# First attention: turning the weighted values with VectorE's 32-square transpose in place of TensorE products with the identity

## The chip, the cores and the metric

The kernel runs on one core of one Trainium2 chip. The metric is device time in microseconds (us) of one execution. The kernel before takes 1176.46 us, the median of three runs between 1171.67 and 1180.38. The profiled execution has a span of 1177.1 us.

Engines are named as in the profile: PE is TensorE (PEld its weight loads), DVE is VectorE, ACT is ScalarE, POOL is GpSimd, SP is the engine whose queue issues most of the DMA. L400 is line 400 of the kernel.

## The reference

The whole program is two layers, each an attention followed by a mixture of experts, on x of 4 batches x 1024 tokens x 256 channels. Only the first attention is touched. Cut to it:

```python
h = _layernorm(x) * (1 + ca) + sa
Q = (h @ Wq.T).reshape(b, t, 16, 16)                 # 16 heads of 16
q_lat = einsum('bthd,hdl->bthl', Q, q_to_latent)     # latent size 64
logits = einsum('bthl,bsl->bhts', q_lat, h @ Wk_down.T) / sqrt(64)
attn = softmax(where(causal, logits, -1e30))
ctx = einsum('bhts,bsl->bhtl', attn, h @ Wv_down.T)
heads = einsum('bhtl,hld->bthd', ctx, v_up)
x = x + ga * (heads.reshape(b, t, 256) @ Wout.T)
```

After it each row of x is normalised again, sent to 2 of 16 experts, and so on. All data is float32.

## The kernel before

**Tiling.** The weights are folded first, so each head has 16 values per token. A batch's heads are worked in four parts: two groups `g` of 128 channels, and within each two halves `o` (the even and the odd heads). A part holds four heads `hh`, one in each quadrant of 32 partitions. The scores are made transposed: keys on partitions, queries along the free axis. A part has nine *units* (`UNITS`), each of 512 query columns of scores for all four heads, so there are 4 x 2 x 2 x 9 = 144 units in all. For a unit PE makes the scores (`ps_s`, L377), ACT takes the exponential (`pT`, L385) and POOL zeroes the part above the diagonal (L388). Two units later PE multiplies with the values (`ps_av`, L457). The values are stored 32 wide: 16 values and then ones, so that the sum of the weights comes out beside the weighted values.

**Where the change sits.** `ps_av` is one PSUM bank (pool `ps_o`, one buffer) of 128 partitions x 512 queries. Its partition is 32 x head + value index, its column is the query. A part fills it twice (`qc` = 0 and 1: the first and the second 512 queries). Two things have to follow: division by the sum, which in this layout lies in another partition than the values, and the output projection, whose stationary operand needs channels on partitions. The kernel before does this in two turns over the identity. First (`finish`, L396 to L408) DVE copies `ps_av` to `oT` (L464), PE turns it in four products with the identity (`ps_oT`, L400), and DVE takes the reciprocal of the sums (L403) and multiplies (L407), which leaves `on` with tokens on partitions. Then (`project`, L410 to L437) for each two tiles of 128 tokens PE turns `on` back in four products with the identity (`ps_onT`, L417), DVE copies the result to `onT` (L426), PE multiplies with the gated output weights (`ps_out`, L431) and DVE adds it to x (L436). Over four batches that is 32 times `finish` and 16 rounds of `project`.

**Order.** `sums()` emits the products of `ps_av` in the order of the parts. Everything beside the scores and sums is a *task*: a generator that yields after each piece (1 or 0.5 a piece). The tasks are `prepare` (normalisation, values, queries and keys of the next group), `finish`, `project`, the rows and routing for the experts (`rows`), and the sort of the routed rows (`sort`). After each unit `k.around.step(...)` runs one piece, and two on every third unit of the batches after the first (L490). Each call of `step` also advances one *rider*: the sending of sorted rows by POOL's indirect DMAs (L944), which begins when `sort` of the first two batches is done. A scheduler places instructions within each engine's queue from there; POOL's queue follows the written order. Each engine works off its queue in order.

**What stands at the end of the attention.** After the last unit come the last sums, the last `finish`, and `project` of batch 3. Then the expert stage begins with `ps_xT` (L1193), which needs the sorted rows of the first two batches to have been sent and read back.

Of the kernel before, what the change touches and what calls it, by code (L numbers as in the profile page):

```python
# [8 lines left out]
F32 = mybir.dt.float32  # L9
I32 = mybir.dt.int32  # L10
AF = mybir.ActivationFunctionType
ALU = mybir.AluOpType
# [3 lines left out]
P = 128  # L16
B, N, C = 4, 1024, 256
NT = N // P
CC = C // P
H, D, L = 16, 16, 64  # L20
# [44 lines left out]
def bcast(ap, axis, n):  # L65

    shape = list(ap.shape)
    shape.insert(axis, n)
    return ap.unsqueeze(axis).to_broadcast(shape)
# [171 lines left out]
def attention0(ctx, k, a, after_batch=lambda b: None):  # L241

    nc = k.nc
    k.scalar_norm = False

    wp = ctx.enter_context(k.tc.tile_pool(name="a0_w", bufs=1, reuse_waits="tile"))
    vs, ons, qs = ([None, None] for _ in range(3))
    par = wp.tile([P, 2], F32, tag="par", name="par")
    wo = wp.tile([P, CC, C], F32, tag="wo", name="wo")
    for i in (1, 0):  # L250
        if i:
            vs[i] = wp.tile([P, NT, H, 32], F32, tag="v1", name="v1")
        ons[i] = wp.tile([P, NT, C], F32, tag=f"on{i}", name=f"on{i}")
        qs[i] = [wp.tile([P, N], F32, tag=f"{n}{i}", name=f"{n}{i}") for n in ("qT", "kT0_", "kT1_")]
    k.xn = wp.tile([P, 4, C], F32, tag="ln_xn", name="ln_xn")
    wq, wk, wv = (wp.tile([P, CC, C], F32, tag=n, name=n) for n in ("wq", "wk", "wv"))
# [29 lines left out]
    misc = Spread()  # L286
# [39 lines left out]
    recs = k.recs  # L326
# [3 lines left out]
    def prepare(b, g):  # L330

        if g == 0:
            yield from layer_norm_steps(k, b, hT, 0, misc, "m")
            for t in range(0, NT, 2):
                ps = misc.tile([P, 2, C], F32, name="ps_v")
                for i in range(2):
                    for cc in range(CC):
                        nc.tensor.matmul(  # L338
                            ps[:, i, :], lhsT=hT[:, cc, (t + i) * P : (t + i + 1) * P],
                            rhs=wv[:, cc, :], start=cc == 0, stop=cc == CC - 1,  # L340
                        )
                nc.scalar.copy(
                    vs[b % 2][:, t : t + 2, :, :D], ps.rearrange("p t (h d) -> p t h d", d=D)
                )
                yield 1
        else:
            gates[b] = spread_rows(k, work, 0, GATE, 0, "gate_a0", b, 1)[:, 0]
        qT, *kTs = qs[g]
        for w in (wq, wk):
            for hf in range(2):  # L350
                ps = misc.tile([P, 512], F32, name="ps_qk")
                for cc in range(CC):
                    nc.tensor.matmul(  # L353
                        ps, lhsT=w[:, cc, g * P : (g + 1) * P],
                        rhs=hT[:, cc, hf * 512 : (hf + 1) * 512],
                        start=cc == 0, stop=cc == CC - 1,
                    )
                cols = slice(hf * 512, (hf + 1) * 512)
                if w is wq:
                    nc.vector.tensor_copy(qT[:, cols], ps)  # L360
                else:
                    for o in range(2):
                        nc.vector.tensor_scalar(  # L363
                            kTs[o][:, cols], ps, par[:, o : o + 1], None, ALU.mult
                        )
                yield 1
        ready[b, g] = qT, kTs
# [25 lines left out]
            pTs.append(pT)  # L393
        return pTs

    def finish(b, g, o, qc, oT, on):  # L396

        pt = misc.tile([P, 4, P], F32, name="ps_oT")
        for i in range(4):
            nc.tensor.transpose(pt[:, i], oT[:, i * P : (i + 1) * P], k.ident)  # L400
        pt = pt.rearrange("p i (j d) -> p i j d", d=32)
        rec = recs[:, 8 * b + 4 * g + 2 * o + qc]
        nc.vector.reciprocal(rec, pt[:, :, :, D])  # L403
        heads = on[:, 4 * qc : 4 * qc + 4, g * P : (g + 1) * P].rearrange(
            "p t (j o d) -> p o t j d", o=2, d=D
        )
        nc.vector.tensor_tensor(heads[:, o], pt[:, :, :, :D], bcast(rec, 3, D), ALU.mult)  # L407
        yield 1  # L408

    def project(b, on):  # L410
        wg = work.tile([P, CC, C], F32, tag="wg", name="wg", bufs=1)
        nc.vector.tensor_tensor(wg, wo, bcast(gates.pop(b), 1, CC), ALU.mult)
        for t in range(0, NT, 2):
            pt = misc.tile([P, 2, CC, P], F32, name="ps_onT")
            for i in range(2):
                for cc in range(CC):
                    nc.tensor.transpose(  # L417
                        pt[:, i, cc, :], on[:, t + i, cc * P : (cc + 1) * P], k.ident
                    )
            if misc.early:  # L420
                onT = work.tile([P, 2, 512], F32, tag="pT", name="onT", bufs=7)[:, 0, :].rearrange(
                    "p (i c n) -> p i c n", c=CC, n=P
                )
            else:
                onT = work.tile([P, 2, CC, P], F32, tag="onT", name="onT", bufs=1)
            nc.vector.tensor_copy(onT, pt)  # L426
            yield 1
            py = misc.tile([P, 2, C], F32, name="ps_out")
            for i in range(2):
                for cc in range(CC):  # L430
                    nc.tensor.matmul(  # L431
                        py[:, i, :], lhsT=onT[:, i, cc, :], rhs=wg[:, cc, :],
                        start=cc == 0, stop=cc == CC - 1,
                    )
            xs = k.x[b][:, t : t + 2, :]
            nc.vector.tensor_tensor(xs, xs, py, ALU.add)  # L436
            yield 1  # L437
# [5 lines left out]
    around = k.around.tasks  # L443

    def sums():

        for b in range(B):
            on = ons[b % 2]
            for g in range(2):
                for o in range(2):  # L450
                    for qc, pieces in enumerate(SUMS):
                        po = ps_o.tile([P, 512], F32, tag="o", name="ps_av")
                        for n, (u, i) in enumerate(pieces):
                            yield place[b, g, o, u]
                            kb, _, c0, w, _ = UNITS[u][i]
                            for hh in range(4):
                                nc.tensor.matmul(  # L457
                                    po[32 * hh : 32 * hh + 32, 512 - w :],
                                    lhsT=vs[b % 2][:, kb, 8 * g + 2 * hh + o, :],
                                    rhs=exps[b, g, o, u][hh // 2][:, hh % 2, c0 : c0 + w],  # L460
                                    start=n == 0, stop=n == len(pieces) - 1,
                                )
                        oT = work.tile([P, 512], F32, tag="oT", name="oT")
                        nc.vector.tensor_copy(oT, po)  # L464
                        around.insert(0, finish(b, g, o, qc, oT, on))
            projects.append(project(b, on))
            around.append(projects[-1])
            after_batch(b)
# [6 lines left out]
    with k.tc.manual_schedule(engines={mybir.EngineType.Pool}):  # L475
        summing = sums()
        wanted = next(summing)
        for n, (b, g, o, u) in enumerate(units):
            if n == 8:
                k.clear_rows()  # L480
            if (o, u) == (0, 0):
                while (b, g) not in ready:
                    k.around.step(rides=0)
                coming = (b, 1) if g == 0 else (b + 1, 0)
                if coming[0] < B:
                    around.insert(0, prepare(*coming))
            while wanted is not None and wanted <= n - 2:
                wanted = next(summing, None)
            exps[b, g, o, u] = scores(b, g, o, u)
            k.around.step(2 if b and n % 3 == 2 else 1)  # L490
        misc.early = True
        for _ in summing:
            pass
        while projects[-1] in around:
            k.around.step(rides=2)
# [1468 lines left out]
def two_layers(ctx: ExitStack, tc: tile.TileContext, a: dict, out: bass.AP):  # L1964
# [83 lines left out]

    load_x(0)
    again = stages(attention0, attention1, True)  # L2050


# [73 lines left out]
```

## Time and profile before

| | PE | DVE | ACT | POOL |
|---|---|---|---|---|
| busy, us of 1177.1 | 1022.0 | 642.4 | 611.9 | 331.4 |
| share of the span | 87% | 55% | 52% | 28% |

| time | us |
|---|---|
| median of three runs | 1176.46 |
| first scores of the attention to the first `ps_xT` of the experts | about 52 to 569.24 |
| PE busy between 52 and 546 | 478.5 of 494 |

A busy share is an average over stages. What matters for a change inside the attention is which engine is never without work there, and which waits end last between two of its instructions. In the lines that follow, a row of the timeline merges equal instructions that follow each other: start, length, engine, line, operation, tiles written and read, count, and in brackets how long the engine had been idle and what released it. A float32 product is recorded as two matmuls, a turn over the identity as one.

### The profile page before, as it was taken

What the parts mean: (1) busy time and instruction counts of PE and PEld (TensorE: products, weight loads), DVE (VectorE), ACT (ScalarE), POOL (GpSimd) and SP (SyncE); (2) the same over time, 40 slices, a digit from 0 to 9 for tenths busy, and PEclk for the clock granted to TensorE, in tenths of its full rate; (3) what the DMA queues carried; (4) which work ended last, traced back from release to release, by engine and by line L of the source; (5) the groups of instructions that cost most, each with busy time, mean ns of one, the idle gap of its engine ahead of it and who ended that gap; (6) DMA issues with size and microseconds to landing.
All of it is one profiled execution on the core that took longest, in us unless ns stands there. A gap on an engine that the chain in (4) does not pass through costs nothing.

```text
span 1177.1 us, 19004 instructions
## 1 busy us (share of the span) xinstructions
PE 1022.0 (87%) x6350; PEld 607.1 (52%) x6350; DVE 642.4 (55%) x2143; ACT 611.9 (52%) x986; POOL 331.4 (28%) x528
## 2 busy tenths in 40 slices
PE   4999999999999998998688999887798798868771
PEld 2533434343444433443567888776465555546651
DVE  5822233422362144441776787896589978685352
ACT  0377645664457445474264757655664745523331
POOL 1122222220112122466104604420461100542732
PEclk9999999999999998998889999998899899889986
DMA  6992000100010000264744655531421501357863
GB/s 190 347 346 82 1 1 1 41 1 1 1 37 24 1 1 1 68 218 176 299 126 158 208 165 170 158 108 54 143 77 35 193 1 45 104 162 226 275 223 107
DMA packets 99017, 134.63 MB, mean 114 GB/s; under 512 B 8744, under 2 KB 86088, under 8 KB 98400
## 3 DMA queue, kind: packets, MB, share of 16 engines
q1 hardware_dynamic: 86528, 98.97, 25.3%
q0 software_dynamic: 11776, 33.57, 9.3%
q8 instruction: 54, 0.88, 0.3%
q10 hardware_dynamic: 608, 0.79, 0.2%
q14 instruction: 51, 0.42, 0.1%
HBM read 69.55 MB, written 63.75 MB: 113 GB/s over the span
## 4 chain that ended last, share of the span: by engine, by line
PE 66%; DVE 16%; DMA 6%; ACT 5%; issue 4%; POOL 1%; DVEq 0%; SPq 0%; POOLq 0%; ACTq 0%
PE ps_av L457 13%; PE ps_s L377 12%; PE ps_y L1282 6%; PE ps_qk L353 5%; PE ps_k L1472 4%; PE ps_h L1216 4%; DMA ys<-results,index 3%; PE ps_v L338 3%; PE ps_out L431 3%; PE ps_pr L1570 2%; PE ps_q L1498 2%; PE ps_oT L400 2%; PE ps_y L1893 2%; DMA xs<-sorted 2%; PE ps_lnT L1034 1%
## 5 line engine op out<-in xcount | busy, mean ns | idle before, releaser
L385 ACT ACTIVATE pT<-ps_s 128x1024 f32<-128x1024 f32 x288 | 278.8, 1021 | 199.8 <-PE ps_s L377 197.2
L388 POOL TENSOR_SCALAR_AFFINE_SELECT pT<-pT 128x256 f32<-128x256 f32 x256 | 101.1, 414 | 394.3 <-ACT pT L385 390.3
L457 PE MATMUL ps_av<-pT,v 128*32 128x512 f32 (+3 forms) x1536 | 180.0, 509 | 3.3 <-POOL pT L388 3.3
L377 PE MATMUL ps_s<-qT,kT 32*128 32x512 f32 (+3 forms) x1536 | 181.7, 524 | 0.5 <-ACT pT L385 0.5
L954 POOL DMA_INDIRECT ys<-results,index x96 | 100.7, 1048 | 139.5 <-DVE st L1227 35.1
L944 POOL DMA_INDIRECT sorted<-hs,index x96 | 96.9, 1009 | 142.5 <-PE ps_y L1282 67.6
L377 PEld LDWEIGHTS ps_s<-qT,kT 32*128 32x128 f32 x1536 | 75.8, 186 | 99.3 <-issue 80.2
L1282 PE MATMUL ps_y<-w,act 128*128 x376 | 93.2, 404 | 20.1 <-ACT act L1265 20.0
L1240 ACT ACTIVATE hid<-hid,nmr,rstd 128x256 f32<-128x256 f32 x94 | 49.0, 595 | 83.8 <-DVE nmr L1236 83.7
L1282 PEld LDWEIGHTS ps_y<-w,act 128*128 128x128 f32 x376 | 74.1, 202 | 33.4 <-ACT act L1265 22.9
L1216 PE MATMUL ps_h<-w,xT 128*128 x376 | 87.8, 386 | 1.6 <-ACT xT L1199 1.5
L457 PEld LDWEIGHTS ps_av<-pT,v 128*32 128x32 f32 x1536 | 41.0, 110 | 90.7 <-issue 64.5
L464 DVE COPY oT<-ps_av 128x512 f32<-128x512 f32 x32 | 22.0, 689 | 114.6 <-PE ps_av L457 114.6
L1216 PEld LDWEIGHTS ps_h<-w,xT 128*128 128x128 f32 x376 | 70.5, 193 | 11.5 <-ACT xT L1199 2.3
L1893 PE MATMUL ps_y<-we,xT 128*128 x212 | 58.3, 422 | 18.3 <-ACT xT L1888 17.8
L1265 ACT ACTIVATE act<-ps_hT,gain 128x128 f32<-128x128 f32 x188 | 67.6, 461 | 4.7 <-PE ps_hT L1256 4.7
L1472 PE MATMUL ps_k<-wqkv,hT 128*128 128x512 f32 x128 | 62.5, 606 | 3.9 <-DMA wqkv<-in_wqkv_dram 3.0
L1893 PEld LDWEIGHTS ps_y<-we,xT 128*128 128x128 f32 x212 | 41.8, 208 | 28.1 <-ACT xT L1888 22.0
L1291 DVE TENSOR_TENSOR y<-ps_y,b 128x256 f32<-128x256 f32 x94 | 37.7, 419 | 23.1 <-PE ps_y L1282 22.9
L101 DVE BATCH_NORM_STATS2 ln_st<-x 128x6 f32<-128x256 f32 x128 | 49.2, 409 | 0.5
L1224 DVE TENSOR_TENSOR hid<-ps_h,b 128x256 f32<-128x256 f32 x94 | 36.4, 414 | 21.4 <-PE ps_h L1216 19.3
L363 DVE TENSOR_SCALAR kT<-ps_qk,par 128x512 f32<-128x512 f32 x32 | 22.5, 746 | 35.9 <-PE ps_qk L353 35.8
(222 smaller groups left out, 1577.6 us busy)
## 6 DMA issues: line engine op xcount, KB each, us to landing
xs<-sorted SPq DMA_DIRECT2D x71, 256.0 KB, 3.8
results<-y SPq DMA_DIRECT2D x71, 256.0 KB, 2.6
sorted<-zero SPq DMA_DIRECT2D x2, 6016.0 KB, 21.6
rows_in<-h SPq DMA_DIRECT2D x16, 512.0 KB, 3.0
hs<-rows_in POOLq DMA_DIRECT2D x32, 256.0 KB, 3.4
w<-in_w_dram SPq DMA_DIRECT2D x8, 1024.0 KB, 10.0
x<-in_x_dram SPq DMA_DIRECT2D x4, 1024.0 KB, 6.4
b<-in_b_dram SPq DMA_DIRECT2D x2, 2048.0 KB
```

The lines of the kernel that those rows point to most:

```text
L353: nc.tensor.matmul(ps, lhsT=w[:, cc, g * P : (g + 1) * P], rhs=hT[:, cc, hf * 512 : (hf + 1) * 512], start=cc == 0, stop=cc == CC - 1,)
L377: k.anchor = nc.tensor.matmul(pair[hh // 2][:, hh % 2, c0 : c0 + w], lhsT=kTs[o][rows, kb * P : (kb + 1) * P], rhs=qT[rows, q1 - w : q1], ...
L385: nc.scalar.activation(pT, ps, AF.Exp, scale=1.0 / L**0.5)
L388: nc.gpsimd.affine_select(out=pT[:, :, c0 : c0 + P], in_=pT[:, :, c0 : c0 + P], compare_op=ALU.is_ge, fill=0.0, base=0, pattern=[[0, 2], [ ...
L457: nc.tensor.matmul(po[32 * hh : 32 * hh + 32, 512 - w :], lhsT=vs[b % 2][:, kb, 8 * g + 2 * hh + o, :], rhs=exps[b, g, o, u][hh // 2][:, h ...
L944: i = self.k.nc.gpsimd.indirect_dma_start(out=buffer.ap, out_offset=bass.IndirectOffsetOnAxis(ap=index, axis=0), in_=rows, in_offset=None, ...
L954: self.paced(self.k.nc.gpsimd.indirect_dma_start(out=rows, out_offset=None, in_=buffer.ap, in_offset=bass.IndirectOffsetOnAxis(ap=index, a ...
L1216: mm = nc.tensor.matmul(ph[:, j], lhsT=xTs[i // 2][:, j, cc], rhs=w1[:, cc, bass.ds(at[i + j], C)], start=cc == 0, stop=cc == CC - 1,)
L1265: o = nc.scalar.activation(act[:, j, cc], pt[:, j, cc], AF.Gelu, bias=gain[:, 1, cc, t : t + 1], scale=gain[:, 0, cc, t : t + 1],)
L1282: mm = nc.tensor.matmul(po[:, j], lhsT=acts[i // 2][:, j, cc], rhs=w2[:, cc, bass.ds(at[i + j], C)], start=cc == 0, stop=cc == CC - 1,)
L1472: k.anchor = nc.tensor.matmul(ps, lhsT=hT[:, cc, t * P : (t + 1) * P], rhs=wqkv[:, cc, C:], start=cc == 0, stop=cc == CC - 1,).ins
L1893: k.anchor = nc.tensor.matmul(po[:, j], lhsT=xT[:, j, cc], rhs=self.we[:, cc, bass.ds(at[j], C)], start=cc == 0, stop=cc == CC - 1,).ins
```

## The change

Both turns move to DVE, whose transpose turns each square of 32 x 32 on its own. `ps_av` is read by one transpose of 128 x 512 straight from PSUM into `turned`: within each quadrant tokens are now on partitions, with the values and the sum of a token side by side. Reciprocal and multiplication follow from there, and write both halves `o` interleaved into `mixed`, so that 32 neighbouring values are the 32 channels of one pair of heads. After the second half a second transpose turns `mixed` back into `onT`, channels on partitions, which is what the projection needs as it stands. The aim is to relieve PE of the products with the identity, and PSUM and DVE of what served them.

With them go the copies `oT` and `onT` and the four-row rounds of `project`. `finish` is no longer a task that waits for its turn, but runs at once after the sums. `on` changes its layout (channels on partitions) but not its size, `mixed` adds two buffers, and the pacing of the tasks is set anew because there are fewer pieces.

```diff
+    mixed = [wp.tile([P, 16, 2, D], F32, tag=f"mixed{qc}", name="mixed") for qc in range(2)]
...
-        ons[i] = wp.tile([P, NT, C], F32, tag=f"on{i}", name=f"on{i}")
+        ons[i] = wp.tile([P, CC, N], F32, tag=f"on{i}", name=f"on{i}")
...
-    def finish(b, g, o, qc, oT, on):
-
-        pt = misc.tile([P, 4, P], F32, name="ps_oT")
-        for i in range(4):
-            nc.tensor.transpose(pt[:, i], oT[:, i * P : (i + 1) * P], k.ident)
-        pt = pt.rearrange("p i (j d) -> p i j d", d=32)
-        rec = recs[:, 8 * b + 4 * g + 2 * o + qc]
-        nc.vector.reciprocal(rec, pt[:, :, :, D])
...
-        nc.vector.tensor_tensor(heads[:, o], pt[:, :, :, :D], bcast(rec, 3, D), ALU.mult)
-        yield 1
+    def finish(b, g, o, qc, po, onT):
+
+
+        turned = work.tile([P, 16, 32], F32, tag="turned", name="turned")
+        nc.vector.transpose(turned.rearrange("p n d -> p (n d)"), po)
+        rec = recs[:, 8 * b + 4 * g + 2 * o + qc].rearrange("p i j -> p (i j)")
+        nc.vector.reciprocal(rec, turned[:, :, D])
+        nc.vector.tensor_tensor(mixed[qc][:, :, o], turned[:, :, :D], bcast(rec, 2, D), ALU.mult)
+        if o == 1:
+            nc.vector.transpose(
+                onT[:, g, qc * 512 : (qc + 1) * 512], mixed[qc].rearrange("p n o d -> p (n o d)")
+            )
...
-            pt = misc.tile([P, 2, CC, P], F32, name="ps_onT")
-            for i in range(2):
-                for cc in range(CC):
-                    nc.tensor.transpose(
-                        pt[:, i, cc, :], on[:, t + i, cc * P : (cc + 1) * P], k.ident
-                    )
...
-            nc.vector.tensor_copy(onT, pt)
-            yield 1
...
-                        py[:, i, :], lhsT=onT[:, i, cc, :], rhs=wg[:, cc, :],
-                        start=cc == 0, stop=cc == CC - 1,
+                        py[:, i, :], lhsT=onT[:, cc, (t + i) * P : (t + i + 1) * P],
+                        rhs=wg[:, cc, :], start=cc == 0, stop=cc == CC - 1,
...
-                        oT = work.tile([P, 512], F32, tag="oT", name="oT")
-                        nc.vector.tensor_copy(oT, po)
-                        around.insert(0, finish(b, g, o, qc, oT, on))
+                        finish(b, g, o, qc, po, on)
...
-            k.around.step(2 if b and n % 3 == 2 else 1)
+            k.around.step(2 if b in (1, 2) and n % 4 == 3 else 1)
```

More of the change, by code (lines that the diff above doesn't have):

```diff
@@ L394, in scores, with project @@
         return pTs
-    def finish(b, g, o, qc, oT, on):
-        pt = misc.tile([P, 4, P], F32, name="ps_oT")
-        for i in range(4):
-            nc.tensor.transpose(pt[:, i], oT[:, i * P : (i + 1) * P], k.ident)
-        pt = pt.rearrange("p i (j d) -> p i j d", d=32)
-        rec = recs[:, 8 * b + 4 * g + 2 * o + qc]
-        nc.vector.reciprocal(rec, pt[:, :, :, D])
-        heads = on[:, 4 * qc : 4 * qc + 4, g * P : (g + 1) * P].rearrange(
-            "p t (j o d) -> p o t j d", o=2, d=D
-        )
-        nc.vector.tensor_tensor(heads[:, o], pt[:, :, :, :D], bcast(rec, 3, D), ALU.mult)
-        yield 1
-    def project(b, on):
+    def finish(b, g, o, qc, po, onT):
[8 more added lines that the diff above has]
+            )
+    def project(b, onT):
         wg = work.tile([P, CC, C], F32, tag="wg", name="wg", bufs=1)
@@ L413, in project @@
         for t in range(0, NT, 2):
-            pt = misc.tile([P, 2, CC, P], F32, name="ps_onT")
-            for i in range(2):
-                for cc in range(CC):
-                    nc.tensor.transpose(
-                        pt[:, i, cc, :], on[:, t + i, cc * P : (cc + 1) * P], k.ident
[L419 to L426, printed above, removed]
-            yield 1
             py = misc.tile([P, 2, C], F32, name="ps_out")
```

## The prediction

> **What bounds the kernel now.** I read the page's engine shares first, then cut the attention into stretches, then followed single boundaries in the timeline. In the stretches the columns are stretch, length, then busy us (instructions) of PE, PEld, DVE, ACT and POOL, then PE's clock:
>
> ```profile
> 98.00:148.00 50.00, 49.73 (x423) 22.46 (x422) 13.49 (x44) 35.00 (x39) 11.47 (x30) 1.00 0.00 1
> 198.00:248.00 50.00, 47.94 (x433) 20.36 (x425) 21.83 (x59) 34.72 (x39) 10.93 (x28) 0.97 0.08 25
> 348.00:398.00 50.00, 49.91 (x420) 22.89 (x417) 10.11 (x23) 35.61 (x40) 12.43 (x32) 1.00 0.10 31
> 546.00:569.00 23.00, 17.94 (x75) 11.53 (x72) 8.33 (x20) 1.70 (x2) 12.62 (x17) 0.70 0.41 135
> ```
>
> PE has work for 48 to 50 of every 50 us; DVE stands at 10 to 22, ACT at 35, POOL at 12. So in the attention an instruction taken off PE is time off the span, unless something else then holds PE up. The last row is the end of the attention: a lower clock and 5 us of idle PE.
>
> The tile's own view gives the turns to be removed, and the waits for them:
>
> ```profile
> L400 PE MATMUL ps_oT<-ident,oT x128: 272/273/477, 65.4 to 556.1; 128*128 128x128 f32 x128
> L464 DVE COPY oT<-ps_av 128x512 f32<-128x512 f32 x32 | 22.0, 689 | 114.6 <-PE ps_av L457 114.6
> PE ps_oT L400 <- DVE oT L464: 9.1, 8, 2.0
> ```
>
> The 273 ns are latency; what a group costs PE is read from the starts in the timeline of an ordinary boundary between two fillings of `ps_av`:
>
> ```profile
> 135.14 0.64 PE L457 MATMUL ps_av<-pT,v 128*32 128x256 f32 x8
> 135.71 1.14 PE L377 MATMUL ps_s<-qT,kT 32*128 32x512 f32 x8
> 135.85 0.69 DVE L464 COPY oT<-ps_av 128x512 f32<-128x512 f32 x1 [7.87 <-PE ps_av L457]
> 136.78 0.66 PE L400 MATMUL ps_oT<-ident,oT 128*128 128x128 f32 x4
> 137.37 1.50 PE L457 MATMUL ps_av<-pT,v 128*32 128x512 f32 x16
> ```
>
> Four turns hold PE from 136.78 to 137.37: 0.59 us. The copy (135.85 to 136.54) lies wholly beside the scores of the next unit. That is the window in which `ps_av`, a single buffer, must be emptied.
>
> The end of the attention on PE and POOL:
>
> ```profile
> 547.08 0.33 PE L417 MATMUL ps_onT<-ident,on 128*128 128x128 f32 x1
> 550.69 1.49 PE L457 MATMUL ps_av<-pT,v 128*32 128x384 f32 x4 [3.28 <-POOL pT L388]
> 558.31 5.99 PE L431 MATMUL ps_out<-wg,onT 128*128 128x256 f32 x16 [0.88 <-DVE onT L426]
> 565.68 3.72 PE L431 MATMUL ps_out<-wg,onT 128*128 128x256 f32 x16 [0.51 <-DVE onT L426]
> 569.24 1.04 PE L1193 MATMUL ps_xT<-ident,xs 128*128 128x128 f32 x8
> ...
> 549.46 0.75 POOL L1134 DMA_DIRECT2D hs<-rows_in  x1 [2.10 <-DMA sorted<-hs,index]
> 550.21 1.48 POOL L388 TENSOR_SCALAR_AFFINE_SELECT pT<-pT 128x256 f32<-128x256 f32 x4
> ```
>
> The last masks stand behind row sending in POOL's queue, PE waits 3.28 us, and then runs its projection with turns in between.
>
> [...] No transpose of DVE is in this trace, [...] 128x128 takes 291 ns (L791), 128x512 takes 689 ns (L464), so 1.04 ns an element. [...] after the 3.28 us wait the clock of that stretch is 0.70.
>
> **Part by part.**
>
> *PE, removed.* 32 groups of `ps_oT` and 16 of `ps_onT`, 48 in all. From start to the next PE row nearly every one takes 0.58 to 0.59 us in the timeline. 48 x 0.585 = 28.1 us, all on the path. The projection's products (128 records) stay.
>
> *PE waits, moved.* The 9.1 us for `oT` come from eight places where DVE was still busy with other tasks when `ps_av` was full. Now the first product of the next filling waits for the transpose itself, since that frees the bank. Queued behind it on PE are the sums, the next scores, and with these ACT's exponentials. In the instruction order of the changed program, of 31 boundaries 12 have the next scores alone between the old and the new filling, 2 more only a short routing product, and the others a task piece of 0.6 us or more. In front of the transposes there is less on DVE than before: only the first (four `kT` scalings, as before: 0.46), one with four `ln_xn` and one with four h operations (4 x 0.48 us beside a window of 1.07) look like a wait. I allow 3.5 us: 5.5 saved.
>
> *DVE.* Removed: 32 copies of 0.689 and 16 of 0.690, 33.1 us. Added: 48 transposes of 128x512. [...] Reciprocal and multiplication read SBUF in place of PSUM: 0.257 and 0.424 before, 0.245 (L810) and 0.41 (L1116) for such shapes from SBUF. So DVE's load stays within 1 us of what it was, and hides beside PE as it did. At 0.71 us the transpose ends at 136.56 in the boundary above, before the scores do at 136.78: no new wait.
>
> *ACT.* The exponentials hide behind PE only as long as PE's unit is longer. A unit without any task has 1.07 (scores) + 1.00 (sums) = 2.07 us on PE and 1.94 on ACT; three `ps_s` buffers make PE wait a little for ACT (score rows of 1.39 against 1.14 at 91.02). A part of nine bare units with two `ps_oT` groups takes 21.51 us (L400 at 79.89 to 101.40), so 20.3 without them, 2.26 a unit. After the units with turns ACT shows idle time of 0.88 and 1.30, so most of the 0.59 comes through. I give back 0.2 in half of the 32: 3 us.
>
> *Pacing.* With fewer pieces the tasks run ahead: the sort of the first two batches is done some 13 units earlier (the first row sending stands after 192 of 256 masks, not 218), and all 32 sendings stand ahead of the last 6 masks, where before 8 stood behind the last. So POOL is free at the end.
>
> *The end.* Counted from the last scores (544.47): exponentials and masks to +4.1, the last sums to +5.1, then 30 of 32 records of `ps_out` at 0.22 us (16 from 565.68 to 569.24) to +11.8, against 24.8 before. DVE's chain of transpose, reciprocal, product, transpose (2.1 us) hides behind the projection of the first 512 tokens. That is 13 us; less five groups of turns that are counted already (2.9) it is 10, and 7 if the projection runs at a clock of 0.7. I take 8. The expert weights needed first were loaded at 516, the rows are sent earlier than before, and the second weights, released by the last `ps_out`, are first used 34 us after `ps_xT`: no new wait. From there on everything moves forward unchanged.
>
> Sum: 28.1 + 5.5 + 8 - 3 = 38.6. 1176.5 - 38.6 = 1138.
>
> **The rivals.**
>
> *Half-rate transposes* (1.24 us). Each of 14 bare boundaries then waits about 0.4 us (136.78 against 137.09 and a semaphore), 6 us, and DVE's extra 25 us collide with tasks for some 3: 1147. For it: no float32 transpose is in the trace. [...]
>
> *ACT takes the bound.* The freed time lies in bare units, and there are more of them in a row at both ends of the attention. If half of the 32 x 0.585 is lost (9 in place of 3), the end gains nothing beyond its turns (8 less) and the old waits stay (5.5 less), 38.6 - 6 - 8 - 5.5 = 19 are left: 1157. For it: the 1.39 us scores. Against: ACT's idle time after the turns.
>
> *Slower: quarter-rate transposes* (2.3 us). 14 bare boundaries wait 1.4 us (20), those with 0.6 us of filling 0.8 (5), DVE's extra 77 us hold up the tasks that PE waits for (10), the old waits double (9): 44 against 38.6, 1182.
>
> **How the numbers follow.** The forecast has 0.72, half rate 0.12, ACT 0.10, the slower case 0.06. The forecast's own bounds are 1129 (no wait left, end 10, nothing to ACT) and 1147. The range, 1127 to 1158, takes in half rate and ACT and leaves out the slower case and what lies beyond my sizes. Faster by over 1% is below 1164.7: forecast, half rate and most of ACT, 0.92. Of the rest 0.05 falls within 1% and 0.03 beyond.
>
> **What would show it.** Right: transposes of 0.69 to 0.75 us, no rows on `ps_oT`/`ps_onT` in this attention, PE's waits before `ps_av` for `turned` of a few us in all, nine bare units in 20 to 21 us, the first `ps_xT` near 531. Wrong: transposes over 1 us; PE's idle time before `ps_av` or `ps_s` growing by more than 10 us; or a first `ps_xT` at 531 with a span above 1150, which would put a loss into the experts.

## The result, and the profile after

| | median us | lowest to highest | ratio to before | 95% interval |
|---|---|---|---|---|
| before | 1177.70 | 1171.67 to 1180.38 | | |
| after | 1119.92 | 1116.60 to 1121.99 | 0.9514 | 0.9469 to 0.9558 |

The change takes 57.8 us off, where 38.6 were forecast; the time lies 7 us below the range. A second set of the same kernel on another chip gave 1119.64 against 1173.45 (ratio 0.9541, 0.9528 to 0.9555). Chips differ by up to 1% in the kernel before, so every run below is set against the kernel before on its own chip. Medians leave out two slow executions, one of the kernel before at 1193.62 us and one of experiment 2 at 1462.92 us with a clock of 0.64.

First, the tile's own view of what was added: count, then shortest/median/longest ns, first and last start.

```profile
L401 DVE STREAM_TRANSPOSE turned<-ps_av x32: 702/716/718, 63.2 to 503.6; 128x512 f32<-128x512 f32 x32
```

A transpose takes 713 ns on average, beside 689 for DVE's copy of that shape (L464 before); the prediction's 0.71 us was my estimate. The other 16, from SBUF, take 711. No row on `ps_oT` or `ps_onT` is left in this attention. How a boundary between two fillings of `ps_av` looks now, in the timeline of PE:

```profile
83.42 1.35 PE L378 MATMUL ps_s<-qT,kT 32*128 32x512 f32 x8
84.70 1.50 PE L443 MATMUL ps_av<-pT,v 128*32 128x512 f32 x16
```

and of DVE:

```profile
83.54 0.72 DVE L401 STREAM_TRANSPOSE turned<-ps_av 128x512 f32<-128x512 f32 x1 [5.14 <-PE ps_av L443]
```

The transpose ends at 84.26, the scores beside it only at 84.70, and the next filling starts there with no wait. The 0.59 us of turns that stood between the two are gone. What PE still waits for ahead of the sums, from the view of waits (total us, times, longest), is this:

```profile
PE ps_av L443 <- DVE turned L401: 6.4, 6, 3.2
PE ps_av L443 <- POOL pT L389: 3.3, 2, 1.6
```

The longest, 3.2 us, is not the transpose's alone: it ends at 436.19, and POOL's last mask before it at 436.04.

And the end of the attention on PE:

```profile
500.07 1.38 PE L443 MATMUL ps_av<-pT,v 128*32 128x512 f32 x8
501.38 0.70 PE L417 MATMUL ps_out<-wg,on 128*128 128x256 f32 x2
502.01 1.58 PE L443 MATMUL ps_av<-pT,v 128*32 128x384 f32 x16
503.52 6.74 PE L417 MATMUL ps_out<-wg,on 128*128 128x256 f32 x30
510.10 1.04 PE L1177 MATMUL ps_xT<-ident,xs 128*128 128x128 f32 x8
```

PE runs from the last sums straight through 30 records of projection into the experts. `ps_xT` starts at 510.10; before it was 569.24, and the forecast was 531. From there to the end of the span 604.7 us pass, and 607.9 before: 59.1 of the 62.3 us between the two profiles lie ahead of the experts. (62.3 is more than the 57.8 of the medians, since the profiled execution of the changed kernel is its fastest, 1116.60 us.)

**Where PE's time went.** For each kernel I added up, from the first scores to the first `ps_xT`, the time from the start of each matmul record to the start of the next, by the tile that is written; time with nothing in flight is counted as idle. The last column cuts across the others: it is the time in which PE was granted half of its clock. All in us:

| | stage | idle | scores | sums | turns | `ps_out` | at half clock |
|---|---|---|---|---|---|---|---|
| before | 520.3 | 21.0 | 172.5 | 168.6 | 30.3 | 32.5 | 27.3 |
| after | 462.7 | 13.5 | 169.0 | 154.0 | 0 | 30.3 | 0 |
| after, second set | 465.1 | 12.1 | 170.6 | 156.3 | 0 | 30.3 | 10.2 |

The rows left out stay within 0.3. The turns gave 30.3, idle time 7.5. The surprise is the sums: 1536 records before and after, of the same shapes, and 14.6 us less. Nothing in the forecast speaks of that.

**The clock.** The half clock in the kernel before comes in four stretches, each at or just behind a wait of PE: 3.4 us behind each of two waits of 1.97 us for `oT`, 6.8 at one of 3.42 in the sort, and 13.7 at the 3.28 us wait for the masks at the end. What such a stretch costs shows at one place in the two profiles of the changed kernel, first set and second:

```profile
436.33 1.06 PE L443 MATMUL ps_av<-pT,v 128*32 128x512 f32 x8 [3.21 <-DVE turned L401]
436.49 1.93 PE L443 MATMUL ps_av<-pT,v 128*32 128x512 f32 x8 [3.20 <-DVE turned L401]
```

The program and the wait are the same, but in the second the clock is 0.50 of full speed for 6.8 us, and the same eight records take 1.87 us to the next row in place of 1.00. So the 24.3 us at half clock in which the kernel before had work cost about 12 us, an estimate, and in the changed kernel nothing or about 4. When the clock falls is not shown: of these two equal waits only one has a slow stretch, and two waits of 1.6 to 1.7 us in the kernel before have none.

**What is different about the sums.** A group of sums is four products, one for each head, in four strips of 32 columns of the array (`128*32` in the view); a group of scores is four products in four strips of 32 rows (`32*128`). A float32 product is two records, so a group is eight. Here is the kernel before at two such groups, in PE's timeline:

```profile
180.06 1.04 PE L457 MATMUL ps_av<-pT,v 128*32 128x512 f32 x2
181.04 1.99 PE L431 MATMUL ps_out<-wg,onT 128*128 128x256 f32 x8
182.96 1.06 PE L457 MATMUL ps_av<-pT,v 128*32 128x512 f32 x6
183.95 1.14 PE L377 MATMUL ps_s<-qT,kT 32*128 32x512 f32 x8
185.03 0.66 PE L417 MATMUL ps_onT<-ident,on 128*128 128x128 f32 x4
185.61 1.07 PE L457 MATMUL ps_av<-pT,v 128*32 128x512 f32 x8
186.61 1.14 PE L377 MATMUL ps_s<-qT,kT 32*128 32x512 f32 x8
```

From 185.61 to 186.61 a whole group takes 1.00 us. The group before it is cut: the scheduler placed a piece of the projection between its first product (two records) and the other three (six). The first then takes 0.98 us (180.06 to 181.04) and the other three 0.99 (182.96 to 183.95). All four products together take about as long as one (1.00 beside 0.98 us), so the cut group costs twice: 0.97 us more, about one group. What stands in the cut is `ps_out`, on the whole array (`128*128`). Why the first product no longer shares its time with the other three is not shown; the price is.

In the instruction order of the program before, 27 of 384 groups are cut: 20 of the sums (13 of 512 columns, the others narrower) and 7 of the scores. After it is 8: two narrow ones of the sums and six of the scores. My theory is that this is the part of the gain that the forecast lacks. The rivals are that sums and scores became shorter for another reason: with the turns, with the pacing, or by the clock (in the kernel before 14.8 us of them are at half clock).

### The profile page after: what moved, and what is told of

The parts are those of the page before. It is cut to its first block, busy times and chain, and to the rows that moved or that the text cites. A ratio compares the mean times of both kernels' runs of the same rounds, so it can differ in the third digit from the quotient of the medians.

```text
span 1114.8 us, 18591 instructions
## 1 busy us (share of the span) xinstructions
PE 966.1 (87%) x6158; PEld 578.1 (52%) x6158; DVE 647.1 (58%) x2143; ACT 612.0 (55%) x986; POOL 337.5 (30%) x528
## 4 chain that ended last, share of the span: by engine, by line
PE 63%; DVE 18%; ACT 6%; issue 5%; DMA 5%; POOL 1%; DVEq 0%; SPq 0%; POOLq 0%; ACTq 0%
PE ps_s L378 12%; PE ps_av L443 11%; PE ps_y L1266 6%; PE ps_qk L354 5%; PE ps_k L1456 4%; PE ps_h L1200 3%; PE ps_v L339 3%; PE ps_out L417 3%; PE ps_pr L1554 3%; DMA ys<-results,index 3%; PE ps_y L1877 2%; PE ps_q L1482 2%; PE ps_lnT L1018 1%; DVE ln_st L101 1%; ACT hid L1224 1%
## 5 line engine op out<-in xcount | busy, mean ns | idle before, releaser
L389 POOL TENSOR_SCALAR_AFFINE_SELECT pT<-pT 128x256 f32<-128x256 f32 x256 | 105.7, 438 | 324.0 <-ACT pT L386 319.3
L378 PE MATMUL ps_s<-qT,kT 32*128 32x512 f32 (+3 forms) x1536 | 178.5, 520 | 0.5 <-ACT pT L386 0.5
L443 PE MATMUL ps_av<-pT,v 128*32 128x512 f32 (+3 forms) x1536 | 164.2, 495 | 9.7 <-DVE turned L401 6.4
L401 DVE STREAM_TRANSPOSE turned<-ps_av 128x512 f32<-128x512 f32 x32 | 22.8, 713 | 97.1 <-PE ps_av L443 96.8
L361 DVE COPY qT<-ps_qk 128x512 f32<-128x512 f32 x16 | 11.1, 691 | 79.1 <-PE ps_qk L354 79.0
```

Source lines behind the costliest of these rows:

```text
L378: k.anchor = nc.tensor.matmul(pair[hh // 2][:, hh % 2, c0 : c0 + w], lhsT=kTs[o][rows, kb * P : (kb + 1) * P], rhs=qT[rows, q1 - w : q1], ...
L389: nc.gpsimd.affine_select(out=pT[:, :, c0 : c0 + P], in_=pT[:, :, c0 : c0 + P], compare_op=ALU.is_ge, fill=0.0, base=0, pattern=[[0, 2], [ ...
L443: nc.tensor.matmul(po[32 * hh : 32 * hh + 32, 512 - w :], lhsT=vs[b % 2][:, kb, 8 * g + 2 * hh + o, :], rhs=exps[b, g, o, u][hh // 2][:, h ...
```

## The experiments

**1. Whole groups by themselves.** In both kernels products 2 to 4 of each group are tied behind product 1: a dependence on it, and a high priority, so that nothing comes between. Turns, tasks, pacing and POOL's queue stay.

```diff
+                            first = None
                             for hh in range(4):
-                                nc.tensor.matmul(
+                                with k.tc.high_priority() if first else nullcontext():
+                                    mm = nc.tensor.matmul(
...
+                                first = glued(k, mm, first)
```

`glued` adds the dependence on the first product, of the class `NoSync`; the scores get the same edit.

Expected of the kernel before with whole groups:

> The kernel before with products 2 to 4 of each group of four (one per head) tied right behind product 1; turns, tasks, pacing and POOL's queue as before. 26 of its 27 cut groups become whole (19 of the 20 cut sums, all 7 cut scores), and the tasks' own products stay where they were within a group's length. Theory 'a cut group costs twice': time on the sums falls from 168.6 to 154 to 156 us, on the scores from 172.5 by 3 to 6, idle time by less than 5 either way; 14 to 22 us less in all, ratio to the kernel before 0.981 to 0.988. Rival 'the sums got shorter because the turns and their pieces went, not because groups became whole': sums stay at 166 or more, ratio 0.996 to 1.004.

Expected of the changed kernel with whole groups:

> The changed kernel with the same tie; its last 8 cut groups (six of the scores at 512 columns, one of 384 and one of 128 of the sums) become whole. Theory 'a cut group costs twice': 5 to 9 us less than the changed kernel, ratio to it 0.992 to 0.996, the scores' time from 169.0 to 163 to 166. Rival 'what is left is hidden behind other waits (a transpose, an exponential)': within 2 us of the changed kernel.

Expected of the changed kernel as it is, on the same chip:

> The changed kernel unaltered, on the same chip as these three, to set them against: ratio to the kernel before 0.947 to 0.956 as in its first runs.

Measured, in one set, with before at 1173.45 us:

| | median us | ratio to before | 95% | cut groups |
|---|---|---|---|---|
| before, whole groups | 1160.31 | 0.9899 | 0.9880 to 0.9919 | 1 |
| after | 1119.64 | 0.9541 | 0.9528 to 0.9555 | 8 |
| after, whole groups | 1113.87 | 0.9483 | 0.9470 to 0.9497 | 0 |

| | stage | idle | scores | sums | turns | `ps_out` | at half clock |
|---|---|---|---|---|---|---|---|
| before, whole groups | 503.3 | 25.4 | 167.3 | 153.2 | 30.0 | 31.9 | 23.9 |
| after, whole groups | 457.7 | 13.8 | 164.8 | 153.2 | 0 | 30.3 | 3.4 |

The place shown above, in the kernel before with whole groups:

```profile
182.51 1.06 PE L462 MATMUL ps_av<-pT,v 128*32 128x512 f32 x8
183.51 1.14 PE L379 MATMUL ps_s<-qT,kT 32*128 32x512 f32 x8
184.58 1.99 PE L434 MATMUL ps_out<-wg,onT 128*128 128x256 f32 x8
186.50 1.06 PE L462 MATMUL ps_av<-pT,v 128*32 128x512 f32 x8
```

The projection now stands between groups, and each group of sums takes 1.00 us. With turns and tasks as they were, the sums of the kernel before fall from 168.6 to 153.2 us. The turns are still there, the pacing is the old one, and 11.3 us of the sums are at half clock beside 11.9, so this fall is the cuts and none of the rivals. The whole kernel gains less than the sums and scores do (20.6 us on both): 12 us by the ratio, 17 in the stage of the profiles. The ratio is just short of what I expected (0.981 to 0.988). Part of the 17 belongs to the clock: the profiled execution of the kernel before has a mean clock of 0.939, its nine runs on this chip 0.943 to 0.950. For the rest, PE comes earlier to waits that it had before; the view of waits shows the largest of these, 9.1 in the kernel before:

```profile
PE ps_oT L403 <- DVE oT L470: 11.5, 8, 3.3
```

The changed kernel gains another 6.0 us from its last 8 cuts (difference of the means of five and five runs, 4.1 to 7.9), as expected. It is the fastest version of this study.

That the sums take 153.2 us in both kernels with whole groups is chance. For each group of sums or scores I took its time beyond the usual (the lower quartile of whole groups of its shape at full clock), and added this up, in us, over the cut groups, over the whole groups at half clock, and over the other whole groups, which hold short waits that don't show as idle time. (The first group of scores, which a product of the setup cuts in every kernel, is among the cut ones here.)

| | cut groups | half clock | other whole groups |
|---|---|---|---|
| before | 22.5 | 6.4 | 12.3 |
| after | 6.6 | 0 | 16.7 |
| before, whole groups | 0.7 | 6.8 | 13.5 |
| after, whole groups | -0.2 | 1.6 | 16.1 |

So from before to after the cuts give 15.9 us on PE and the clock 6.4, and the short waits take 4.4 back. Not all of the 15.9 reaches the span, as the whole kernels above show.

**2. Cutting groups on purpose.** The base is the changed kernel with PE's queue kept in the written order too (experiment 3), which has no cuts. One turn of the identity, whose result is not used, goes into each of the 32 fillings of `ps_av`: in one kernel between products 1 and 2 of the first group, in the other ahead of product 1.

```diff
                             for hh in range(4):
+                                if n == 0 and hh == 1:      # the other kernel: hh == 0
+                                    pt = misc.tile([P, 4, P], F32, name="ps_one")
+                                    nc.tensor.transpose(pt[:, 0], k.ident, k.ident)
                                 nc.tensor.matmul(
```

Expected with the cut:

> The changed kernel with kept PE order and one turn of the identity put into each of the 32 fillings of the sums' bank, between the first and the second of the four products of its first group (all 512 columns wide); nobody reads the turn. It cuts 32 groups in two. Cut groups: 32 x (0.98 + 0.15 to 0.25 for the turn itself) = 36 to 39 us above the changed kernel with kept order (1143), 1177 to 1184. Rival 'it was the waits and the order, not the cut': 32 x 0.15 to 0.25, 1148 to 1151.

Expected without it:

> The same 32 turns of the identity, put ahead of the first product of each filling, so that no group is cut. Cut groups: 32 x 0.15 to 0.25 = 5 to 8 us above the changed kernel with kept order, 1147 to 1152, and 28 to 33 us below the kernel with the cut groups. Rival: the two kernels with 32 turns agree within 5 us.

Measured, with before at 1184.87: 1181.86 us with the cut (ratio 0.9984, 0.9962 to 1.0006), 1173.25 without (0.9903, 0.9875 to 0.9931). PE's timeline with the cut:

```profile
108.22 1.04 PE L446 MATMUL ps_av<-pT,v 128*32 128x512 f32 x2
109.19 0.33 PE L445 MATMUL ps_one<-ident 128*128 128x128 f32 x1
109.45 1.06 PE L446 MATMUL ps_av<-pT,v 128*32 128x512 f32 x6
```

The turn itself takes 0.26 us (109.19 to 109.45). The cut adds the first product's 0.97. Over the stage the sums take 185.1 us against 154.3 in the base: 30.8 for 32 cuts, 0.96 each, as expected. Without the cut they take 155.5. By the ratios, the whole time with the cut is 38 us above the base (0.9664, on another chip), as expected, but without it 28 above in place of 5 to 8. So the two are about 9 us apart, not 28 to 33. Without the cut the turn stands at the head of PE's queue and waits for its PSUM buffer, which the tasks share: 23.7 us idle ahead of it in place of 5.6, and 27.3 us of the stage at half clock in place of 13.7. So this pair shows the price of a cut, and is no clean comparison of whole times; experiment 1 is.

**3. PE in written order.** One edit, in the kernel before and in the changed one, keeps PE's queue as written, so that no group is cut.

```diff
-    with k.tc.manual_schedule(engines={mybir.EngineType.Pool}):
+    with k.tc.manual_schedule(engines={mybir.EngineType.Pool, mybir.EngineType.PE}):
```

Expected of the kernel before:

> The kernel before, with PE's queue in the attention kept in the written order, so that no task stands between the four products of a group of scores or sums (27 of 384 groups are cut in two in the kernel before, 20 of them sums; none here). Theory 'cut groups': the four column tiles of a sums group run side by side, a group cut in two pays twice, 0.98 us for each of 13 cut groups of 512 columns, 0.7 for 4 of 384: this kernel is 13 to 17 us faster than before, 1160 to 1164. Rival 'the turns and waits are worth more than I counted': the order of PE's queue is worth nothing, 1172 to 1181.

Expected of the changed kernel:

> The changed kernel with PE's queue in the attention kept in the written order (8 cut groups in the changed kernel, 2 of them sums; none here). Cut groups: 0 to 3 us faster than the changed kernel, 1115 to 1121, and against the kernel before with kept order (1160 to 1164) the turns and waits alone leave 42 to 47 us. Rival: as before less 57, whatever the order: the same 1117 to 1123, but then the kernel before with kept order stays at 1177.

Measured, with before at 1181.84: 1188.89 us (1.0059, 1.0035 to 1.0083) and 1142.73 us (0.9664, 0.9624 to 0.9705). Both are misses in whole time. The sums do fall as expected, to 152.8 and 154.3 us, but idle time rises from 21.0 to 46.4 and from 13.5 to 27.5, and time at half clock from 27.3 to 37.5 and from 0 to 17.1. The view of waits of the kernel before in this form shows by what:

```profile
PE ps_oT L400 <- DVE oT L464: 11.2, 8, 2.9
PE ps_qk L353 <- DVE qT L360: 6.2, 4, 3.8
```

A task piece that is not ready now stands at the head of the queue, and the next scores wait behind it. The scheduler's freedom removes such waits and pays for it with cuts; the tie of experiment 1 has the one without the other.

**4. The turns put back.** On the changed kernel in written order, PE gets 48 groups of four turns of the identity (results not used) where `ps_oT` and `ps_onT` stood.

```diff
         turned = work.tile([P, 16, 32], F32, tag="turned", name="turned")
+        pt = misc.tile([P, 4, P], F32, name="ps_oT")
+        for i in range(4):
+            nc.tensor.transpose(pt[:, i], k.ident, k.ident)
...
+            pt = misc.tile([P, 4, P], F32, name="ps_onT")
+            for i in range(4):
+                nc.tensor.transpose(pt[:, i], k.ident, k.ident)
             py = misc.tile([P, 2, C], F32, name="ps_out")
```

> The changed kernel with kept PE order and with the 48 groups of four turns over the identity put back on PE, at the same places (after each filling and in each round of the projection); they turn the identity itself, nobody reads them and nobody waits for them. It prices PE's time for the turns alone: 48 x 0.585 = 28 us above the changed kernel with kept order, 1144 to 1150. Rival 'PE has slack there' (ACT's exponentials set the pace in bare units): under 20 us, below 1140. Rival 'turns cost more than their start to start time': over 33 us.

Measured: 1173.48 us (0.9909, 0.9885 to 0.9934), 30.8 over its base of 1142.73, which itself lies above what was expected; the stage is 28.1 longer. The turns' own records take 28.3 us, 0.59 a group. So this term of the sum (28.1) is right, and the change would be worth it for this alone.

**5. The pacing.** The changed kernel with the pacing of before, the changed kernel with one piece a step throughout, and the kernel before with the new pacing:

```diff
-            k.around.step(2 if b in (1, 2) and n % 4 == 3 else 1)
+            k.around.step(2 if b and n % 3 == 2 else 1)      # old pacing
...
+            k.around.step(1)                                 # one piece
```

Expected of the changed kernel with the old pacing:

> The changed kernel with the pacing of the kernel before (a second piece on every third unit of batches 1 to 3). 15 groups are cut, 6 of them sums of 512 columns. Cut groups: 6 x 0.98 less the changed kernel's 1 us, so 4 to 7 us slower than the changed kernel, 1124 to 1127. Rival 'pacing is what frees POOL at the end': the tasks run ahead as much or more here, so the end costs the same and the time is 1118 to 1122.

Expected of the changed kernel with one piece a step:

> The changed kernel with one piece after each unit, never two. One group is cut (8 in the changed kernel), but the first row is sent after 218 masks, as in the kernel before, and 8 sendings stand behind the last mask. Cut groups: 7 us less on PE. The early end of the sendings, which I sized at 10 us with the clock, is lost: PE waits some 3 us for masks and the first rows come later. Together 1118 to 1128 beside the changed kernel's 1120. If sums groups and end were both nothing, 1120.

Expected of the kernel before with the new pacing:

> The kernel before with the pacing of the changed kernel alone (a second piece on every fourth unit of batches 1 and 2). The tasks still hold the 32 pieces of the turns, so they run behind: the first row is sent after 234 masks, 20 sendings stand behind the last. 15 groups are cut against 27. Cut groups: 12 us less on PE up to the last scores. The end: 12 sendings more at 1.28 us behind the last mask, of which the projection hides some, so 5 to 15 us more there. In all 1170 to 1182. Rival 'pacing alone explains the gain': 1150 or less.

| | median us | ratio | 95% | cuts, sums + scores | sums us | scores us | idle us |
|---|---|---|---|---|---|---|---|
| after, old pacing | 1144.42 | 0.9667 | 0.9608 to 0.9726 | 6 + 9 | 164.2 | 176.0 | 15.2 |
| after, one piece | 1140.67 | 0.9628 | 0.9568 to 0.9688 | 1 in all | 156.2 | 165.9 | 24.8 |
| before, new pacing | 1180.09 | 0.9955 | 0.9937 to 0.9972 | 8 + 7 | 156.4 | 169.6 | 25.7 |

The old pacing costs the changed kernel 0.0153 between the ratios, about 18 us, about as much as the time on sums and scores grows (10.2 and 7.0 us). Seven more cuts at 0.96 are 6.7 of these 17.2, so the cuts give the direction and less than half of the size. Most of the rest is the clock, as PE's timeline shows:

```profile
392.07 1.05 PE L443 MATMUL ps_av<-pT,v 128*32 128x512 f32 x2
395.19 1.08 PE L1091 MATMUL ps_gain<-mine,g 16*128 16x47 f32 x4 [2.08 <-DVE offset L914]
...
397.06 1.93 PE L443 MATMUL ps_av<-pT,v 128*32 128x512 f32 x6
398.92 2.09 PE L378 MATMUL ps_s<-qT,kT 32*128 32x512 f32 x8
```

Here it is the sort that cuts a group, and it waits for DVE in the middle of it. After the wait three products take 1.86 us instead of 0.99 and a group of scores about 2 instead of 1.07; the granted clock from 380 to 400 us is 0.87 (0.50 from 395 to 401), where the changed kernel has 1.00. In the whole stage 17.1 us are at half clock, where the changed kernel's first profile has none; 13.9 of them fall on sums and scores and cost about 7 us, an estimate. With the cuts that is 13.7 of the 17.2 us. What is left I have not settled.

One piece a step has the fewest cuts of the three and yet is slower than the changed kernel. Of its waits, these are the largest:

```profile
PE ps_av L443 <- DVE turned L401: 9.7, 5, 3.4
PE ps_xT L1177 <- DVE ln_rstd L90: 6.6, 1, 6.6
```

The tasks fall behind, eight sendings of rows stand after the last mask in POOL's queue, the experts begin with 6.6 us of waiting, and 22.5 us of the stage are at half clock. The kernel before with the new pacing gives its 12 us on the sums back in the same way (10.7 us idle before `ps_xT`, 20 sendings after the last mask). So the pacing has two effects that were expected, cuts and lateness of the rows, and a third, the clock behind the waits, that the expectations counted at the end at most. Only the last expectation held, where cuts and lateness nearly cancel.

**6. The room beside the transpose.** The changed kernel does the transpose of the sums twice in a row.

```diff
         nc.vector.transpose(turned.rearrange("p n d -> p (n d)"), po)
+        nc.vector.transpose(turned.rearrange("p n d -> p (n d)"), po)
```

> The changed kernel with the transpose of the sums done twice in a row, 32 more of 0.713 us on VectorE; order of all engines else unchanged. It asks how much room the transpose has before TensorE feels it, the disputed size of the half-rate rival. The forecast's window (0.7 us of transpose beside 1.07 us of scores, some 0.2 to 0.5 us left): the bank is free 0.7 us later, idle time of TensorE ahead of the sums grows by 6 to 14 us over its 9.7, and the time by as much, ratio to the changed kernel 1.005 to 1.012. Rival 'the release is what PE waits for already at most boundaries': all of it is felt, 32 x 0.71 = 23 us, ratio 1.02. Rival 'the queue has slack': under 3 us.

Measured: 1129.47 us (0.9619, 0.9599 to 0.9639), 9.8 over the changed kernel, within what was expected. The waits ahead of the sums:

```profile
PE ps_av L444 <- POOL pT L389: 9.0, 5, 4.0
PE ps_av L444 <- DVE turned L402: 8.1, 10, 2.2
```

For 22.9 us more of transposes PE sits idle 17.5 us ahead of the sums in place of 9.7: 7.8 more, as expected (6 to 14). The view names POOL in five places, but in three of them (1.1, 1.1 and 4.0 us) the second transpose ends with the last mask or after it (at 445.88 beside 445.68 in the longest). So 14.3 of the 17.5 us are waits in which the transpose is among the last to end, where the changed kernel has 6.4. PE waits so in 13 places, which leaves 18 of the 31 boundaries with room for twice the transpose. The scores' time rises by 1 to 2.5.

## Why the prediction was wrong in size and right in direction

- *Transposes of 0.71 us, DVE's load unchanged:* right. 713 ns is measured, DVE is busy 647.1 us in place of 642.4 (4.7 more, where I had 1), and the rivals of half and quarter rate fall with it. In the trace before only DVE's copies speak for 0.71: 291 ns for 128x128 (L791) and 689 for 128x512 (L464), so 1.04 ns an element; that a transpose keeps this rate was not shown. The rivals' 1.24 and 2.3 us were suppositions too: they are near what twice and four times 1.04 ns an element give on top of the 0.17 us of a 128x8 operation of DVE (L81), an estimate. Experiment 6 shows that a transpose of twice the length would have cost about 10 us, most of it at the boundaries.
- *48 groups of turns at 0.585:* right. 30.3 us go from the stage, 0.63 a group, because 4.7 of them are at half clock; put back they cost 28.3.
- ***The step that failed: the sum had no term for groups that become whole.*** Under "PE, removed" the sums and scores were taken as fixed work. The instruction order that I read for boundaries and sendings also held the cuts: 27 before, 8 after. Made whole by themselves they bring 12.0 us before and 6.0 after (experiment 1, means). So they are worth 6 to 7 us of the difference on that chip: 53.8 us lie between the kernels as they are, 46.4 between those with whole groups (medians). The two pairs of profiles say 12 (57.6 and 45.6 us of stage), but the pairs come from different chips, and the profiled execution of the kernel before has the lower clock.
- ***A second term at nothing: the clock behind PE's waits.*** The working priced a wait at its idle time, and the low clock at the end alone. The lines that it shows held a sign of more: a clock of 0.97 from 198 to 248 us. In the stage before, half of the 27.3 us at half clock lie ahead of the end, about 6.5 us by the estimate above. The runs of experiment 1 agree: their mean clock is 0.946 before and 0.950 after, so that the share of the clock that was not granted, times the span, falls by 7.6 us, the end included. This term is read from traces; no experiment here changes the clock alone.
- *Waits ahead of `ps_av`, 9.1 to 3.5:* mis-sized. `turned` still costs 6.4, in six places, and in the longest (3.2) the masks are as late.
- *The end, 8 us beyond its turns:* mis-sized the other way. From the start of the last record of scores to `ps_xT` it is 23.7 us before and 10.2 after, so 10.5 beyond the 2.9 of turns. The working had 10 and took 8 against a slow clock; the projection's 30 records took 0.22 us each.
- *3 us given back to ACT:* about right, but hidden. In the timeline of DVE the transposes at 76.72 and 97.45 are nine bare units apart: 20.73 us, where the forecast had 20 to 21 and before it was 21.51. Two groups of turns (1.17) brought 0.78, so about 0.2 is lost for each there, as allowed. Over the stage the scores take 2.5 us less with whole groups, not 3 more, because the clock is in that figure too; the table by groups has 2.6 us more of short waits in sums and scores with whole groups, and 4.4 more as they are. That all of these are waits for ACT is not shown.
- *The rivals:* ACT as the bound at 1157 and the slower case at 1182 are both refuted by the time.

With whole groups in both kernels the stage gives 45.6: turns 30.0, idle time 11.6, scores 2.5, `ps_out` 1.6. That is 7.0 above the forecast's 38.6. By the estimate above the low clock costs about 11 us in the first of these two profiles and 1.7 in the second, spread over all of these rows but idle time, and the forecast had only its part at the end; so the clock is of the size of these 7. The cuts come on top. Both work in one direction, which the range did not allow for: the forecast's lower bound of 1129 came from the same terms, each at its best, and had no room for terms that were missing.

## What to carry to other kernels

Where small products share the array in strips, read the instruction order for whole-array instructions between the members of a group: in the timeline it is a row of x2 and one of x6, each as long as an x8 (0.98 and 0.99 us beside 1.00 here). Tying the members together is a small edit that made both kernels faster (12 and 6 us here), and keeping the whole queue in written order is no substitute, since it trades the cuts for waits (46.4 us idle in place of 21.0 in the kernel before). When a change removes or moves tasks, count the cuts before and after, since they can be worth a seventh of what the rest of the change is worth (6 to 7 us beside 46 here). And price a wait of PE with the granted clock behind it (1.87 us in place of 1.00 for a group at a clock of 0.50): read the clock in short stretches, as a mean over the span (0.939 here) hides it.

## What the runs showed of the hardware

- A group of four float32 products in strips (512 columns, 1.00 us) takes hardly longer than one of them alone (0.97 to 0.98), so a whole-array instruction of 0.26 us between them cost 0.96 us more than its own time.
- DVE's transpose of 128x512 float32 takes on average 713 ns from PSUM and 711 from SBUF, within 4% of its copy of that shape (689).
- Behind one and the same wait of 3.2 us a group of sums took 1.00 us in one execution and 1.87 at a clock of 0.50 in another. The kernel before has stretches of half clock behind waits of 1.97 us too.
